# An adaLN + mixture-of-LoRA kernel in Strassen form: a second block on two levels, modulation in place, seeds in PSUM

## The chip, the cores and the metric

One core of one Trainium2 chip. The time is what the device needs for one execution, in microseconds (us); before the change three runs gave a median of 265.66 (265.64 to 265.94). Profiles come from single executions under the hardware profiler. Engines in the profile: PE is TensorE's matmuls, PEld its weight loads, DVE is VectorE, ACT is ScalarE, POOL is GpSimd, SP is SyncE, which here only issues DMAs.

## The reference

All in float32; x is 64 batches of 64 rows of 512.

```python
q_emb = relu(cond_1024 @ W3 + b3)                       # one row of 512 per batch
v = (64 * x + x.sum(axis=1, keepdims=True)) * q_emb[:, None, :]
y = relu(v @ W2 + b2)                                   # first wide product, 512 x 512
base = y @ W_base + b_base                              # second wide product, 512 x 512
shared = (y @ A_s) @ B_s                                # rank 16
gates = softmax(y @ W_router + b_router)                # 6 experts, the best two are kept
routed = sum over experts of w_e * ((y @ A_r[e]) @ B_r[e])
out = x + base + shared + routed
```

## The kernel before

**Blocks.** The 4096 rows are worked in NB = 4 blocks of 16 batches (1024 rows). Features lie on the partitions: a block of x is a tile of 128 partitions x 4 chunks c of features x 2 halves h of the rows x 512 rows. Half 0 has the first 32 rows of each batch, half 1 the others. A block goes through four stages: modulation (x to v), the first wide product (v to y), `ph` (the gate and low-rank products of y, 118 columns), and the second wide product, with the routed part added and the result sent out (`second`).

**Seven products.** Both wide products are Winograd's form of Strassen's scheme: row halves and feature halves make a 2 x 2 of 2 x 2, and seven products of half size take the place of eight. `weight_sums` makes the four sums of weights and `row_sums` the four sums of rows (DVE). `product(ps, i, j, ...)` is product i for output columns j (two j): two matmuls over 512 columns, four records in the trace, 1.72 us. Before the change, block 0 takes half of its rows without sums (`first_mixed`), blocks 1 and 2 take seven products (`first_seven`), and block 3 takes the scheme on two levels (`first_inner`): each of the seven outer products o is again seven inner ones n, 49 matmuls over 256 columns (`q(n, t)`, t counts the outer products in the list `order`). There the common parts of the inner results are carried within PSUM: `seed_y` and `seed_z` copy one bank's half to another with ScalarE, and later matmuls add to it.

**Buffers.** PSUM has eight banks: six for the wide products (`ps_p`), two for `ph` and `pt` (`ps_h`). A bank is asked for with each `ps_p.tile`; one that was used before waits for its last reader. x has three buffers in SBUF and v two; temporaries for results (`temps`: u, u22, u21, u12) have one each.

**Order of the work.** Each engine works its instructions in the order of the program text; there is no scheduler. Modulation of block k+1 runs in the gaps of block k: `prepare(k + 1)` puts its steps in a list `behind`, and `fill(n)` and `share()` in the code of block k take the next steps out. A step is in the main four activations of ScalarE (one per batch) for one chunk, with the next chunk's sums on DVE in front (`sums`: a scaling, a reduction over 1024 elements, a multiplication). `second` takes what is left in nine shares. `prepare_inner` adds the sums that the two-level form needs (inner_t of weights, inner_s of rows).

**Second product.** For each j, product 1 (`x`) is copied to SBUF (L654), added to product 6 (`y`) by DVE (L658), and GpSimd adds x to that three times (L662). `add_r` adds product 7 (`z`). `pt` transposes the weighted low-rank results (`hw`), ScalarE copies them to hwT, and `routed` adds their products to the banks. `finish` (L674) adds bias and remainder and sends 128 x 512 out through SP. The residual x comes from the tile of x, which is why v has its own.

**Loads.** SP issues all loads first, those of x_1 and x_2 at once, and x_3 behind block 0's outputs.

Of the kernel before, what the change touches and what calls it, by code (L numbers as in the profile page):

```python
# [27 lines left out]
NQ = Q // P  # L28
G = E + 1
# [5 lines left out]
def adaln_ffn(ctx: ExitStack, tc: tile.TileContext, xa, x0, x1, head, w3, w2, wb, a, bcat, br, outT):  # L35
# [12 lines left out]
    vpool = ctx.enter_context(tc.tile_pool(name="v", bufs=2))  # L48
    mid = ctx.enter_context(tc.tile_pool(name="mid", bufs=1))
    tmp = ctx.enter_context(tc.tile_pool(name="tmp", bufs=1))  # L50
    tmp1 = ctx.enter_context(tc.tile_pool(name="tmp1", bufs=1))
# [4 lines left out]
    outTv = outT.rearrange("k c h p t -> p c k h t")  # L56
    xs, vs, ss = {}, {}, {}

    def load_x(k):
        xs[k] = xpool.tile([P, NC, 2, TB], F32, tag="x", name=f"x_{k}")  # L60
        for c in range(NC):
            nc.sync.dma_start(xs[k][:, c].rearrange("p h t -> p (h t)"), x1[k - 1, c])
# [4 lines left out]

    def rows(k, f, h):

        return first_rows(f)[:, :, h] if k == 0 else split(xs[k][:, f, h])  # L70

    def split(t, g=2):
        return t.rearrange("p (g n) -> p g n", g=g)
# [50 lines left out]
    load_x(2)  # L124
# [9 lines left out]
    def weight_sums(w, name):  # L134
# [11 lines left out]
        return {1: b11, 2: b21, 3: b22, 4: t[3], 5: t[0], 6: t[1], 7: t[2], "sums": all_t}, steps  # L146

# [25 lines left out]
    def modulate(k):  # L173


        vs[k] = v = vpool.tile([P, NC, 2, TB], F32, tag="v", name=f"v_{k}")
        vsum = small.tile([P, NC, BB], F32, tag="vsum", name=f"vsum_{k}")
        nq = small.tile([P, NC, BB], F32, tag="nq", name=f"nq_{k}")

        def sums(c):  # L180
            xc = xs[k][:, c].rearrange("p h (b n) -> p b h n", n=NH)
            q = q_sb[:, c, ts(k, BB)]
            nc.vector.tensor_scalar(nq[:, c], q, float(N), None, ALU.mult)
            nc.vector.tensor_reduce(vsum[:, c, :], xc, AX.XY, ALU.add)  # L184
            nc.vector.tensor_tensor(vsum[:, c, :], vsum[:, c, :], q, ALU.mult)  # L185

        def batches(c, lo, hi):
            for b in range(lo, hi):
                nc.scalar.activation(  # L189
                    v[:, c, :, ts(b, NH)], xs[k][:, c, :, ts(b, NH)], AF.Identity,  # L190
                    bias=vsum[:, c, b : b + 1], scale=nq[:, c, b : b + 1],
                )

        n = BB // 4
        parts = [(c, lo) for c in range(NC) for lo in range(0, BB, n)]
        steps = [lambda: sums(0)]
        for m, (c, lo) in enumerate(parts):
            if lo == 0 and c + 1 < NC:
                steps.append(lambda c=c, lo=lo: (sums(c + 1), batches(c, lo, lo + n)))
            else:  # L200
                steps.append(lambda c=c, lo=lo: batches(c, lo, lo + n))
        return steps
# [39 lines left out]
    def row_sums(a, name, cols=slice(0, TB)):  # L242

        a11, a12, a21, a22 = a[:, :KH, 0, cols], a[:, KH:, 0, cols], a[:, :KH, 1, cols], a[:, KH:, 1, cols]
        all_s = mid.tile([P, 4, KH, TB], F32, tag=name, name=name)
        s = [all_s[:, i, :, cols] for i in range(4)]
        steps = [
            lambda: nc.vector.tensor_tensor(s[0], a21, a22, ALU.add),
            lambda: nc.vector.tensor_tensor(s[1], s[0], a11, ALU.subtract),
            lambda: nc.vector.tensor_tensor(s[2], a11, a21, ALU.subtract),  # L250
            lambda: nc.vector.tensor_tensor(s[3], a12, s[1], ALU.subtract),
        ]
        return {1: a11, 2: a12, 3: s[3], 4: a22, 5: s[0], 6: s[1], 7: s[2], "sums": all_s}, steps

    def temps(name):
        return {n: tmp.tile([P, KH, TB], F32, tag=n, name=f"{n}_{name}") for n in ("u", "u22", "u21", "u12")}
# [3 lines left out]
    def fill(n):  # L260
        for _ in range(min(n, len(behind))):
            behind.pop(0)()

    def prepare(k):
        behind.extend(modulate(k))
        ss[k], steps = row_sums(vs[k], "s")
        behind.extend(steps)
        if k == NB - 1:
            prepare_inner(k)

    def prepare_inner(k):


        vectors = nc.vector.tensor_tensor
        t_flat = xpool.tile([P, NC, 2, TB], F32, tag="x", name="inner_t").rearrange("p c h t -> p (c h t)")
        at = {i: n for n, i in enumerate((5, 6, 7, 4, 1, 2, 3))}
        inner_t = t_flat[:, : 4 * 7 * P].rearrange("p (n o m) -> p n o m", n=4, o=7)

        def t_of(o, n):
            w, a = t2[o], at[o]  # L280
            b = {1: w[:, 0, :P], 2: w[:, 1, :P], 3: w[:, 1, P:]}
            return b[n] if n in b else inner_t[:, {5: 0, 6: 1, 7: 2, 4: 3}[n], a]

        w_low = w2_sb.rearrange("p (o k) m -> p o k m", k=KH)
        groups = ((slice(0, 4), lambda c, m: t2["sums"][:, :, c, ts(m, P)]),
                  (slice(4, 6), lambda c, m: w_low[:, :, c, ts(m, P)]),
                  (slice(6, 7), lambda c, m: t2[3][:, c, ts(m, P)].unsqueeze(1)))
        t_steps = []
        for o, b in groups:
            t = [inner_t[:, n, o] for n in range(4)]  # L290
            t_steps += [
                lambda t=t, b=b: vectors(t[0], b(0, 1), b(0, 0), ALU.subtract),
                lambda t=t, b=b: vectors(t[1], b(1, 1), t[0], ALU.subtract),
                lambda t=t, b=b: vectors(t[2], b(1, 1), b(0, 1), ALU.subtract),
                lambda t=t, b=b: vectors(t[3], b(1, 0), t[1], ALU.subtract),
            ]
        for n, step in enumerate(t_steps):
            m, other = 2 + n, behind[2 + n]
            behind[m] = lambda step=step, other=other: (other(), step())

        R2 = TB // 2
        s = {}

        def places():
            s["sums"] = vpool.tile([P, NC, 2, TB], F32, tag="v", name="inner_s").rearrange(
                "p c h t -> p (c h t)").rearrange("p (n o t) -> p n o t", n=4, o=4)
            s["first"] = small.tile([P, 4, 1, R2], F32, tag="inner_s1", name="inner_s1")

        def late_places():
            late = mid.tile([P, 4, KH, TB], F32, tag="sy", name="inner_late").rearrange("p n k t -> p (n k t)")  # L310
            s["late"] = late[:, : 8 * R2].rearrange("p (n o t) -> p n o t", n=4, o=2)
            s["e3"] = late[:, 8 * R2 : 12 * R2].rearrange("p (j t) -> p j t", j=KH)

        sources = (("first", lambda c, r: vs[k][:, c, 0, ts(r, R2)].unsqueeze(1)),
                   ("sums", lambda c, r: ss[k]["sums"][:, :, c, ts(r, R2)]),
                   ("late", lambda c, r: vs[k][:, KH + c, :, ts(r, R2)]))
        s_steps = [places]
        for g, a in sources:
            s_steps += [
                lambda g=g, a=a: vectors(s[g][:, 0], a(0, 1), a(1, 1), ALU.add),  # L320
                lambda g=g, a=a: vectors(s[g][:, 1], s[g][:, 0], a(0, 0), ALU.subtract),
                lambda g=g, a=a: vectors(s[g][:, 2], a(0, 0), a(0, 1), ALU.subtract),
                lambda g=g, a=a: vectors(s[g][:, 3], a(1, 0), s[g][:, 1], ALU.subtract),
            ]
        behind.extend(s_steps[:-4])
# [3 lines left out]
        def s_of(o, n):  # L329
# [7 lines left out]
        inner.update(t=t_of, s=s_of, e3=lambda: s["e3"], late=[late_places] + s_steps[-4:])  # L337
# [4 lines left out]
    def first_mixed(y):  # L342
# [3 lines left out]
        vs[0] = v = vpool.tile([P, NC, 2, TB], F32, tag="v", name="v_0")  # L346
# [516 lines left out]
```

## Time and profile before

The profiled execution took 265.05 us: its span from first to last instruction is 263.3, and 1.75 lie around it.

| what | us |
|---|---|
| median of three runs | 265.66 |
| profiled execution / its span | 265.05 / 263.3 |
| TensorE's first `py` matmul starts, last matmul ends | 5.75, 259.3 |
| block 0: `ph` starts, second product starts | 33.4, 40.5 |
| block 1: first product, `ph`, second product start | 72.6, 96.6, 104.2 |
| block 2: the same | 136.0, 160.0, 167.6 |
| block 3: the same | 199.4, 220.4, 227.9 |

How to read it: the page counts each engine's busy time; windows give the same for any stretch, so that a stage of one block can be laid beside that of another. A timeline row gives start, duration, engine, line, operation, output and inputs, count, and in brackets how long the engine had been idle and what it waited for. "The chain of waits" follows the work that ended last back from its end. Some durations worth knowing here:

| row | what | mean ns |
|---|---|---|
| L189 ACT | one batch's modulation, 128x64 | 429 (16 in a row: 5.41 us) |
| L184 DVE | row reduction, 128x1024 | 1212 |
| L662 POOL | add of x, 128x512 | 1356 |
| L674 DVE | bias, PSUM and remainder, 128x512 | 748 |
| L654 ACT | copy out of PSUM, 128x512 | 581 |
| L486, L489 ACT | seed copy within PSUM, 128x256 | 357, 363 |
| x loads, SP | 512 KB | 7.1 us to landing |
| outputs, SP | 256 KB | 2.0 us to landing |

### The profile page before, as it was taken

What the parts mean: (1) busy time and instruction counts of PE and PEld (TensorE: products, weight loads), DVE (VectorE), ACT (ScalarE), POOL (GpSimd) and SP (SyncE); (2) the same over time, 40 slices, a digit from 0 to 9 for tenths busy, and PEclk for the clock granted to TensorE, in tenths of its full rate; (3) what the DMA queues carried; (4) which work ended last, traced back from release to release, by engine and by line L of the source; (5) the groups of instructions that cost most, each with busy time, mean ns of one, the idle gap of its engine ahead of it and who ended that gap; (6) DMA issues with size and microseconds to landing.
All of it is one profiled execution on the core that took longest, in us unless ns stands there. A gap on an engine that the chain in (4) does not pass through costs nothing.

```text
span 263.3 us, 2789 instructions
## 1 busy us (share of the span) xinstructions
PE 257.9 (98%) x920; PEld 148.8 (57%) x920; DVE 168.4 (64%) x296; ACT 119.2 (45%) x318; POOL 43.8 (17%) x45
## 2 busy tenths in 40 slices
PE   7999999999999999999999999999999999999995
PEld 3756895454444458444444447744446889845542
DVE  2896889636755448714667776876989566872422
ACT  2499389594018992245003998246004328101000
POOL 1000000570000000435000000055600070045300
PEclk9999999999999999999999999999999999999999
DMA  6999300004362000002220000000332000000323
GB/s 200 364 346 410 123 0 0 0 2 159 115 249 113 0 2 0 1 0 88 111 105 18 0 0 0 2 0 0 113 128 80 1 4 0 0 4 0 120 90 109
DMA packets 10303, 20.13 MB, mean 76 GB/s; under 512 B 1216, under 2 KB 3008, under 8 KB 10288
## 3 DMA queue, kind: packets, MB, share of 16 engines
q1 hardware_dynamic: 10000, 19.82, 20.7%
q8 instruction: 7, 0.11, 0.2%
q10 hardware_dynamic: 288, 0.13, 0.2%
q14 instruction: 8, 0.07, 0.1%
HBM read 11.56 MB, written 8.39 MB: 76 GB/s over the span
## 4 chain that ended last, share of the span: by engine, by line
PE 91%; ACT 5%; DMA 2%; DVE 1%; SPq 0%; issue 0%; DVEq 0%
PE oz L150 11%; PE ox L150 10%; PE ph L801 10%; PE ow L150 9%; PE py L354 5%; PE yw L150 5%; PE yz L150 5%; PE oy L150 5%; PE ia L480 5%; PE ow L668 5%; PE yx L150 4%; PE ib L480 4%; PE yy L150 3%; ACT v L189 3%; PE ox L668 3%; PE oz L668 3%
## 5 line engine op out<-in xcount | busy, mean ns | idle before, releaser
L189 ACT ACTIVATE v<-x,vsum,nq 128x64 f32<-128x64 f32 x192 | 66.3, 429 | 6.7 <-DVE vsum L185 6.7
L662 POOL TENSOR_TENSOR u_o<-u_o,x 128x512 f32<-128x512 f32 x24 | 31.9, 1356 | 178.3 <-DVE u_o L658 178.3
L801 PEld LDWEIGHTS ph<-a_sb,y 128*128 128x128 f32 x256 | 29.5, 192 | 1.8 <-issue 1.0
L801 PE MATMUL ph<-a_sb,y 128*128 128x118 f32 x256 | 29.9, 276 | 0.3 <-ACT y L340 0.3
L150 PE MATMUL ox<-y,wb_sb 128*128 128x512 f32 x64 | 29.5, 593 | 0.0
L340 ACT ACTIVATE y<-u,head_sb 128x512 f32<-128x512 f32 (+1 forms) x26 | 15.9, 633 | 8.8 <-DVE u L412 3.6
L150 PEld LDWEIGHTS ox<-y,wb_sb 128*128 128x128 f32 x64 | 11.8, 190 | 12.9 <-issue 12.9
L674 DVE SCALAR_TENSOR_TENSOR u_o<-ow,head_sb,u_o 128x512 f32<-128x512 f32 x14 | 10.5, 748 | 8.5 <-PE ow L668 8.2
L658 DVE TENSOR_TENSOR u_o<-oy,op 128x512 f32<-128x512 f32 x8 | 5.5, 688 | 15.5 <-PE oy L150 15.5
L354 PE MATMUL py<-v,w_sb 128*128 128x512 f32 (+1 forms) x40 | 14.4, 510 | 0.9 <-DMA w_sb<-in_w_dram 0.9
L150 PE MATMUL oz<-y,tb 128*128 128x512 f32 x32 | 15.1, 595 | 0.0
L150 PE MATMUL yx<-v,w_sb 128*128 128x512 f32 x32 | 15.0, 592 | 0.0
L150 PE MATMUL oz<-sy,tb 128*128 128x512 f32 x32 | 15.0, 592 | 0.0
L150 PE MATMUL oy<-sy,tb 128*128 128x512 f32 x32 | 15.0, 592 | 0.0
L437 ACT COPY p<-yx 128x512 f32<-128x512 f32 x4 | 2.3, 576 | 27.7 <-PE yx L150 27.7
L184 DVE TENSOR_REDUCE vsum<-x 128x16 f32<-128x1024 f32 x12 | 14.5, 1212 | 0.0
L654 ACT COPY op<-ox 128x512 f32<-128x512 f32 x8 | 4.7, 581 | 19.1 <-PE ox L150 19.1
L150 PE MATMUL ow<-sy,tb 128*128 128x512 f32 x28 | 13.2, 593 | 0.0
L150 PE MATMUL ow<-sy,wb_sb 128*128 128x512 f32 x28 | 13.2, 592 | 0.0
L674 DVE SCALAR_TENSOR_TENSOR x<-ox,head_sb,x 128x512 f32<-128x512 f32 x8 | 6.0, 749 | 10.6 <-PE ox L668 10.6
L486 ACT COPY ib<-ia 128x256 f32<-128x256 f32 x7 | 2.5, 357 | 21.2 <-PE ia L480 21.2
L237 ACT ACTIVATE v<-x,vsum,nq 128x64 f32<-128x64 f32 x32 | 10.9, 427 | 1.7 <-DVE vsum L235 1.7
(170 smaller groups left out, 413.3 us busy)
## 6 DMA issues: line engine op xcount, KB each, us to landing
x<-in_x_dram SPq DMA_DIRECT2D x12, 512.0 KB, 7.1
out_dram<-u_o SPq DMA_DIRECT2D x22, 256.0 KB, 2.0
out_dram<-x SPq DMA_DIRECT2D x8, 256.0 KB, 2.1
x<-in_x_dram SPq DMA_DIRECT2D x7, 256.0 KB, 6.0
w_sb<-in_w_dram SPq DMA_DIRECT2D x4, 256.0 KB, 5.7
wb_sb<-in_wb_dram SPq DMA_DIRECT2D x4, 256.0 KB, 5.0
w_sb<-in_w_dram SPq DMA_DIRECT2D x1, 384.0 KB, 4.3
out_dram<-u_o SPq DMA_DIRECT2D x2, 192.0 KB, 1.9
```

What stands on the lines that cost most here:

```text
L150: nc.tensor.matmul(ps, w[i][:, c, ts(j, P)], s[i][:, c, :], start=start and c == 0, stop=c == KH - 1, skip_group_check=True,)
L184: nc.vector.tensor_reduce(vsum[:, c, :], xc, AX.XY, ALU.add)
L189: nc.scalar.activation(v[:, c, :, ts(b, NH)], xs[k][:, c, :, ts(b, NH)], AF.Identity, bias=vsum[:, c, b : b + 1], scale=nq[:, c, b : b + 1],)
L237: nc.scalar.activation(v[:, c, :, ts(b, NH)], batches_of(c, b, b + 1)[:, :, 0], AF.Identity, bias=vsum[:, c, b : b + 1], scale=nq[:, c, b ...
L340: nc.scalar.activation(y[:, f, h, cols], src, AF.Relu, bias=b2_sb[:, f : f + 1])
L354: nc.tensor.matmul(p[:, :, lo * NH : hi * NH], w2_sb[:, c, ts(f, P)], v[:, c, :, lo * NH : hi * NH], start=(c == 0 and lo == 0), stop=(c = ...
L480: nc.tensor.matmul(bank[b, t][:, cols], inner["t"](o, n), inner["s"](o, n), start=n == 1, stop=True, skip_group_check=True,)
L658: nc.vector.tensor_tensor(us[j], ps["y", j], p1s[j], ALU.add)
L662: nc.gpsimd.tensor_tensor(split(t[j], x.shape[1]), split(us[j], x.shape[1]), x, ALU.add)
L668: nc.tensor.matmul(ps[name, j], bcat_sb[:, ts(f, P)], hw, start=False, stop=True, skip_group_check=True)
L674: nc.vector.scalar_tensor_tensor(add, split(p, g), bb_sb[:, f : f + 1], add, ALU.add, ALU.add)
L801: nc.tensor.matmul(ph[:, h * NS + s, :HC], y[:, c, h, ts(s, P)], a_sb[:, c, :], start=(c == 0), stop=(c == NC - 1),)
```

## The change

- **First product of block 2** is `first_inner` too, with its own row sums; the weight sums inner_t are constants and are made during block 1. `first_inner` itself now has fills (two units ahead of step t = 2, two in each step), since block 3 is prepared behind it. The four sums of the group `late` are GpSimd's and come first.
- **Modulation in place**: v is the tile of x. A unit is two activations instead of four; chunks go in the order 0, 2, 1, 3, and the row sums are made in halves.
- **The residual** is loaded a second time: `load_rows(k)`, behind the first product, into the four temporaries (512 KB each). `with_x` adds bank and bias to it.
- **Seeds**: in `first_seven` and `second` ScalarE copies a bank into a fresh bank and the next product adds to it, in place of a copy to SBUF and adds on DVE and GpSimd. Relus read PSUM where they can. The order of products in `second` is new.
- **Block 0**: the accumulators of j = 0 and j = 1 share a bank (`px`, and `y`, `w`, `z` of the seven products).
- x_2 is loaded behind block 0's modulation, x_3 behind `load_rows(0)`.

```diff
     def load_x(k):
         xs[k] = xpool.tile([P, NC, 2, TB], F32, tag="x", name=f"x_{k}")
-        for c in range(NC):
-            nc.sync.dma_start(xs[k][:, c].rearrange("p h t -> p (h t)"), x1[k - 1, c])
+        for c in CHUNKS:
+            nc.sync.dma_start(xs[k][:, c].rearrange("p h t -> p (h t)"), x1[k, c])
...
-        vs[k] = v = vpool.tile([P, NC, 2, TB], F32, tag="v", name=f"v_{k}")
+        vs[k] = v = xs[k]
...
+        def batch(c, b):
+            x = v[:, c, :, ts(b, NH)]
+            nc.scalar.activation(x, x, AF.Identity, bias=vsum[:, c, b : b + 1], scale=nq[:, c, b : b + 1])
...
     def fill(n):
         for _ in range(min(n, len(behind))):
-            behind.pop(0)()
+            for step in behind.pop(0):
+                step()
-    def prepare(k):
+    def prepare(k, also=()):
...
+        early, late = row_steps(slice(0, 1)), row_steps(slice(1, 2))
+        units = [[sums[CHUNKS[0]]]]
+        for i, c in enumerate(CHUNKS):
+            for b in range(0, BB, 2):
+                unit = batches[c][b : b + 2]
+                if b == 0 and i + 1 < NC:
+                    unit.insert(0, sums[CHUNKS[i + 1]])
+                if i == KH and b % 4 == 2:
+                    unit.append(early[b // 4])
+                units.append(unit)
+        for n, step in enumerate(also):
+            units[2 + n].append(step)
+        behind.extend(units + [[step] for step in late])
+        if k > 1:
+            behind.extend([step] for step in prepare_inner(k))
...
+        late = [late_places] + steps("late", lambda c, r: vs[k][:, KH + c, :, ts(r, R2)], nc.gpsimd)
...
     def first_mixed(y):
...
-                    px[j], w2_sb[:, c, ts(j, P)], v[:, c, 0, other], start=(c == 0), stop=(c % KH == KH - 1),
+                    px[:, j], w2_sb[:, c, ts(j, P)], v[:, c, 0, other],
+                    start=(c == 0 and j == 0), stop=(c % KH == KH - 1),
...
-                    nc.scalar.copy(p1[j], px[j])
+                    nc.scalar.copy(p1[j], px[:, j])
...
+        load_x(2)
...
+        banks = [ps_p.tile([P, KH, cols], F32, tag="pp", name=f"y{n}_0") for n in "ywz"]
...
     def first_seven(k, y):
         s = ss[k]
-        prepare(k + 1)
+        prepare(k + 1, inner_steps)
...
             product(px, 1, j, t2, s)
-            nc.scalar.copy(p1, px)
-            product(py, 6, j, t2, s)
-            nc.vector.tensor_tensor(u, py, p1, ALU.add)
-            fill(1)
+            nc.scalar.copy(py, px)
             product(pw, 5, j, t2, s)
-            nc.vector.tensor_tensor(r, pw, u, ALU.add)
-            fill(1)
-            product(pz, 7, j, t2, s)
+            nc.scalar.copy(r, pw)
+            product(py, 6, j, t2, s, start=False)
+            nc.scalar.copy(pz, py)
+            product(px, 2, j, t2, s, start=False)
+            nc.scalar.copy(u, py)
+            fill(2)
+            relu(y, f1, 0, px)
+            product(pz, 7, j, t2, s, start=False)
             nc.vector.tensor_tensor(r, pz, r, ALU.add)
+            fill(2)
             relu(y, f2, 1, r)
-            fill(2)
-            product(px, 2, j, t2, s, start=False)
-            relu(y, f1, 0, px)
             product(pw, 3, j, t2, s, start=False)
             nc.vector.tensor_tensor(r2, pw, u, ALU.add)
+            fill(2)
             relu(y, f2, 0, r2)
-            fill(1)
             product(pz, 4, j, t2, s, start=False)
-            nc.vector.tensor_tensor(r1, pz, u, ALU.add)
-            relu(y, f1, 1, r1)
-            fill(1)
+            relu(y, f1, 1, pz)
+            fill(2)
...
     def first_inner(k, y):
-        late = inner["late"]
-        late.pop(0)()
+        for step in inner[k]["late"]:
+            step()
+        prepare(k + 1)
...
-        for step in late:
-            step()
         q(2, 0)
...
         q(2, 1)
+        fill(2)
         for t in range(2, 7):
...
             take_w5(t)
+            fill(1)
             q(3, t - 1)
...
                 relus(p1, 0, 0)
+            fill(1)
...
+    def load_rows(k):
+        res = {}
+        for n, (f, h) in zip(pair_tags[2:3] + pair_tags[:2] + pair_tags[3:], ((1, 0), (1, 1), (0, 0), (0, 1))):
+            res[f, h] = tmp.tile([P, KH, TB], F32, tag=n, name=f"x{n}_{k}")
+            nc.sync.dma_start(
+                res[f, h], x1[k, f * KH : (f + 1) * KH, :, ts(h, TB)].rearrange("c p t -> p c t")
+            )
+        return res
...
+        def seed(name, source, j):
+            nc.scalar.copy(bank(name, j), ps[source, j])
...
+        def with_x(name, j, f, h):
+            t = row(f, h)
+            nc.vector.scalar_tensor_tensor(t, ps[name, j], bb_sb[:, f : f + 1], t, ALU.add, ALU.add)
+            return t
...
+        def leave(p, f, h, add, cols=slice(0, TB), queue=nc.sync):
+            nc.vector.tensor_tensor(add[:, cols], p[:, cols], add[:, cols], ALU.add)
+            queue.dma_start(outT[k, f, h, :, cols], add[:, cols])
...
         prod(1, 0, "x")
-        copy_p1(0)
-        prod(6, 0, "y")
-        add_u(0)
+        seed("y", "x", 0)
+        prod(1, 1, "x")
+        seed("y", "x", 1)
+        prod(6, 0, "y", start=False)
+        seed("z", "y", 0)
+        prod(2, 0, "x", start=False)
...
+        u12[0] = with_x("y", 0, KH, 0)
         share()
-        prod(7, 0, "z")
-        prod(2, 0, "x", start=False)
-        add_r(0)
-        prod(1, 1, "x")
-        copy_p1(1)
+        prod(7, 0, "z", start=False)
+        u22[0] = with_x("z", 0, KH, 1)
+        prod(6, 1, "y", start=False)
+        seed("z", "y", 1)
+        u12[1] = with_x("y", 1, KH + 1, 0)
         share()
-        prod(4, 0, "z", start=False)
-        prod(6, 1, "y")
-        add_u(1)
-        share()
-        prod(7, 1, "z")
+        prod(2, 1, "x", start=False)
+        prod(7, 1, "z", start=False)
+        u22[1] = with_x("z", 1, KH + 1, 1)
...
+        share()
+        prod(4, 0, "z", start=False)
         prod(5, 0, "w")
-        add_r(1)
...
-        elif k < NB - 1:
+        elif k == 1:
             first_seven(k, y)
         else:
             rest = first_inner(k, y)
+        res = load_rows(k)
+        if k == 0:
+            load_x(3)
...
         if k == 0:
-            fill(4)
-        second(k, y, ph)
-        if k + 3 < NB:
-            load_x(k + 3)
+            fill(8)
+        second(k, y, ph, res)
```

## The prediction

> **What bounds the kernel now.** I read part 1 of the page first, then the same stages of different blocks side by side in windows, then the timelines around every place where TensorE idles.
>
> ```profile
> PE 257.9 (98%) x920; PEld 148.8 (57%) x920; DVE 168.4 (64%) x296; ACT 119.2 (45%) x318; POOL 43.8 (17%) x45
> ```
>
> TensorE is busy for 257.9 of 263.3 us, and 3.9 of the rest lie behind its last matmul. No other engine is near a bound as a sum, so the change can gain in two ways only, by fewer matmul columns or by the few waits of TensorE, and it loses by each new wait of TensorE. Columns of the windows below: stretch, its length, busy time (instructions) of PE, PEld, DVE, ACT, POOL, granted clock, DMA share, GB/s.
>
> ```profile
> 33.40:40.55 7.15, 7.15 (x66) 7.15 (x65) 6.47 (x11) 6.56 (x20) 0.00 (x0) 1.00 0.00 0
> 40.55:72.60 32.05, 32.05 (x83) 14.43 (x82) 20.61 (x35) 17.97 (x53) 8.67 (x7) 1.00 0.17 58
> 96.60:104.20 7.60, 7.43 (x66) 7.25 (x65) 5.42 (x5) 3.59 (x10) 0.00 (x0) 1.00 0.01 2
> 104.20:136.00 31.80, 31.80 (x82) 14.49 (x82) 17.00 (x28) 9.12 (x25) 8.67 (x7) 1.00 0.16 58
> 136.00:160.00 24.00, 24.00 (x58) 10.60 (x57) 16.26 (x31) 17.21 (x45) 0.00 (x0) 1.00 0.03 11
> 160.00:167.60 7.60, 7.43 (x66) 7.25 (x65) 5.61 (x6) 3.60 (x10) 0.00 (x0) 1.00 0.01 2
> 199.40:228.00 28.60, 28.60 (x164) 25.62 (x163) 20.45 (x41) 13.16 (x34) 5.00 (x4) 1.00 0.05 16
> ```
>
> The rows are: block 0's gate matmuls (`ph`), its second product; block 1's `ph`, its second product; block 2's first product with seven products, its `ph`; block 3's first product on two levels together with its `ph`. The reader sees three differences between equal work. Block 2 takes 24.00 + 7.60 = 31.60 where block 3 takes 28.60. `ph` takes 7.60 in blocks 1 and 2 but 7.15 in block 0. Block 0's second product takes 32.05, block 1's 31.80.
>
> **What goes, by those rows.** Block 2 takes the form of block 3: 31.60 - 28.60 = **3.00** (about 2.55 from 24.5 instead of 28 matmuls of 512 columns, 0.45 from the wait in `ph`). Block 1 keeps seven products; its 0.45 in `ph` is this wait (shown for block 2):
>
> ```profile
> 160.24 1.43 ACT L189 ACTIVATE v<-x,vsum,nq 128x64 f32<-128x64 f32 x4
> 161.56 0.71 ACT L340 ACTIVATE y<-u,head_sb 128x512 f32<-128x512 f32 x1
> 162.32 5.39 PE L801 MATMUL ph<-a_sb,y 128*128 128x118 f32 x46 [0.17 <-ACT y L340]
> ```
>
> The last relu stands on ScalarE behind four modulation activations and, before them, behind DVE's add. In the new order that relu reads PSUM directly and stands ahead of the last fill, and the one before it is behind four activations that fit between: with the third product from the end done 3.43 before the end T, DVE's add ends at T-2.7, relu to T-2.05, four activations (0.334 from start to start, 16 in 5.41) to T-0.7, relu to T. The first `ph` group needs it 0.65 later. So **0.45** goes, and row sums and gate follow with room. Block 0's 0.25 is product 4 of j=0, which waited for DVE's add behind GpSimd's L662; it now comes two products later, and L662 is gone: **0.25**. Sum of gains 3.70.
>
> **What is added, one by one.** Seeds in the second product: a 128x512 ScalarE copy out of PSUM took 581 ns (L654; 256 wide, to PSUM 357, to SBUF 378, so 0.55 to 0.6). Each seed has a product of 1.72 between its source and its user. Gate's exponential stands ahead of the first seed; it ended 1.0 behind `ph` in blocks 1 and 2, and 2.65 in block 0: there copy to 3.25, and TensorE asks at 3.44. Cost 0, but the cover in block 0 is 0.2; a later gate is paid one to one. The seed of z for j=1 is queued behind the first share's eight activations (2.76): from 5.8 to 8.6 behind `ph`, and its source ends at 10.3. Cover 1.7, cost 0. hwT's copies are behind the second share, which ends at 13.7, and `pt` at 14.6: 0. ScalarE's four copies and four relus per half of block 1 (about 4.4) plus 14 to 16 activations (5) fit in 12.0 of matmuls: 0.
>
> The reload of x: four 512 KB loads per block on SP, each behind the release of a temporary; the nearest row, 512 KB loads of x, landed in 7.1. The first piece is asked for about 12 us behind the start of `ph`, its buffer is free at or before that start, and no output is queued behind a load that waits long. 8 MB more at a mean of 76 GB/s: 0 (bounds 0 and 1). The moved loads of x for blocks 2 and 3 go out behind x_0's last reader (22.4) and behind block 0's first product (about 36), at least 35 us before block 2 and 3 read them. Modulation in place is the same instruction, `leave` as a plain add is no dearer than L674's 749 ns: 0. The twelve weight sums move into block 1 (0.28 to 0.69 each, 6 in all) and the row sums are cut in halves (8 x 0.69 for 4 x 1.22): DVE is busy 12 of 24 there, 0.
>
> Block 0's **shared banks** are the first place where rule and row part. `px` for j=0 and j=1 now lie in one PSUM bank.
>
> ```profile
> 22.41 0.81 ACT L367 COPY p<-yx 128x256 f32<-128x256 f32 x2
> 22.84 1.59 PEld L361 LDWEIGHTS yx<-v,w_sb 128*128 128x128 f32 x8 [0.43 <-ACT p L367]
> ```
>
> With a bank each, the first copy ran beside j=1's matmuls and TensorE went on after it, at 22.84. By this row the cost is 0. The Trainium skill (PSUM — Partial Sum Buffer, section on bank collisions) says that two engines must be kept apart on a whole bank, whatever columns they touch, so both copies come after both matmuls (22.81) and the next matmul after both copies: 22.85 + 0.37 + 0.37 = 23.57 instead of 22.84, **0.7**. Here the rule speaks against the change, and block 3 agrees with it: its seed copy of the low half of a bank starts at 205.03, behind the matmul into the other half (from 204.40), not behind its own. I take 0.7.
>
> **Fills in block 2's two-level product.** Write S for its start (199.53 in block 3, in the chain of waits). The ninth matmul ends at S+4.2, DVE's take of it at S+4.6. Behind it DVE now has two chunk sums (0.17 + 1.21 + 0.17, about 1.45 each), and ScalarE's first two activations need the first: S+6.05. Then two activations (0.67), a copy (0.27), the seed (0.36): S+7.4. TensorE wants that seed at S+6.75 (206.29 in block 3). Cost **0.66**. Later steps fit: per step ScalarE has two seeds and four activations, about 1.9, in 3.0 of matmuls. At the end two activations (0.67) stand ahead of the relus of e3, which had 0.3 to spare: **0.3**.
>
> **`late` moves to GpSimd**, the second such place. Four 128x512 adds (nearest L575: 1.27 each) start there when `sy` is free, at S-0.86; DVE then still has two 1024-wide sums and the last `leave` (0.75): the product before the last ends at S-2.6, its `leave` at S-1.85, and the ninth share puts three sums of 1.22 (L321 to L323) behind it. Whose bank matters: the third step opens the fifth and sixth bank at S+4.6, one of which that `leave` must have freed.
>
> ```profile
> 180.62 5.69 POOL L662 TENSOR_TENSOR u_o<-u_o,x 128x512 f32<-128x512 f32 x3 [4.22 <-DVE u_o L658]
> 180.95 2.02 DVE L248 TENSOR_TENSOR s<-v 128x1024 f32<-128x1024 f32 x1 [0.41 <-ACT v L189]
> 189.29 1.21 DVE L251 TENSOR_TENSOR s<-v,s 128x1024 f32<-128x1024 f32 x1
> ```
>
> Beside GpSimd the wide add took 2.02 instead of 1.21 (L249 and L250: 1.69, 2.28; mean +0.8). By this row the two sums run from S-0.65 to S+3.4, `leave` to S+4.15: free in time, cost 0. The skill (SBUF — State Buffer, Who interferes with whom) calls it an exclusive lock: an add with two SBUF inputs waits for a whole GpSimd add. Taking turns, `leave` ends at S+4.85, and blocks 2 and 3 wait 0.25 each. I take the row; the rule's 0.5 stays in the range.
>
> **Sum.** 3.70 - 0.70 - 0.66 - 0.30 = 2.04. The profiled execution took 265.05 (span 263.3 and 1.75 around it), so 263.0. The median of the runs shown is 265.66, 0.61 above the profiled one; against it I forecast **263.6**.
>
> **Rivals.**
> - *The costs don't come* (the banks are kept apart by columns only, DVE gets to its sums early): 265.66 - 3.70 = 262.0. Against it: the 205.03 row. Chance 0.12.
> - *ScalarE sets the pace of block 2's first product.* An activation alone lasts 429 ns, not 334. From one seed to the next stand 0.36 + 2 x 0.43 = 1.22, against 1.29 of matmuls (three of 0.43), so any further 0.1 to 0.3 per handover is TensorE's wait. Over five steps 1.7 at most: 265.3, no change. For it, thin cover; against it, 16 activations in 5.41. Chance 0.13.
> - *Slower: GpSimd holds DVE in both two-level blocks.* GpSimd starts first, and if three of its adds go ahead of DVE's two sums, these begin at S+2.95, end at S+5.4, `leave` at S+6.1. The third step then waits 1.5 in block 2 and in block 3, and block 2's sums come 0.4 later still: 3.4 more, 267.0. It eats the whole gain once `leave` ends at about S+5.5. For it: POOL was 1.5 times slower in that stretch too, so both wait; against it: DVE never waited for more than one add there. I put other waits on seeds (block 0's 0.2 of cover) here as well. Chance 0.25.
> - The forecast itself, with its own range 262.5 to 264.9 by the bounds above: 0.50.
>
> A measurement of this kernel can tell about 0.2%, 0.53 us, from no change. Faster by more: the forecast and the first rival, less the edge, 0.60. Within: 0.13. Slower: 0.27. The range 261.7 to 266.7 takes in all but the upper part of the slower case.
>
> **What would show it.** Right: block 2's first product with `ph` at 29.5 to 30 in the windows, `ph` of block 1 at 7.15, about 0.7 of TensorE idle at 22.8 to 23.6 ended by ACT L367's copy, one wait of some 0.7 for the seed in block 2's third step, seconds at 31.8. Wrong: TensorE waits for ScalarE copies inside the second products, for a bank at S+4.6 behind DVE's last `leave`, or for a residual load.

## The result, and the profile after

The changed kernel takes **267.03 us** (median of four runs, 266.89 to 267.27) where the kernel before took 265.65 beside it: ratio 1.0053, 95% interval 1.0036 to 1.0070. The forecast was 263.6; the change is slower by 1.4. (In the later rounds the kernel before took 267.3 to 267.7 in 16 of 89 executions, for a reason that no trace here shows; its medians stay at 265.63 to 265.66, and the table of stages below accounts for the 1.4.) The profiled execution took 267.05 (span 265.0). Part 1 of its page:

```profile
PE 256.7 (97%) x962; PEld 157.2 (59%) x962; DVE 177.8 (67%) x327; ACT 133.7 (50%) x356; POOL 31.3 (12%) x33
```

TensorE has less to do than before (256.7 against 257.9), yet the span grew by 1.7: the gain in matmuls was given back as waits. The windows tell in which stages (columns as before: stretch, length, busy time of PE, PEld, DVE, ACT, POOL, clock, DMA share, GB/s):

```profile
41.64:73.45 31.81, 31.81 (x83) 14.43 (x82) 21.87 (x39) 19.83 (x57) 1.27 (x1) 1.00 0.43 161
97.48:104.61 7.13, 7.13 (x65) 7.13 (x64) 4.72 (x4) 2.21 (x6) 0.00 (x0) 1.00 0.67 220
136.42:167.57 31.15, 29.11 (x164) 25.46 (x162) 25.67 (x47) 20.28 (x56) 11.44 (x8) 1.00 0.23 78
199.37:229.77 30.40, 28.84 (x163) 25.54 (x162) 22.81 (x38) 13.16 (x34) 12.25 (x8) 1.00 0.25 84
```

The rows are block 0's second product, block 1's `ph`, and the first product with `ph` of blocks 2 and 3. The first two are full and as short as forecast. The last two do the same matmuls as block 3 did before in 28.57, and TensorE stands still in both. By the starts of TensorE's stages, in us (block 0's first product counted from its first `yx` matmul to `ph`):

| stage | before | after | difference |
|---|---|---|---|
| block 0, `yx` to `ph` | 15.89 | 16.59 | +0.70 |
| block 0, second product | 32.05 | 31.81 | -0.24 |
| block 1, `ph` | 7.56 | 7.13 | -0.43 |
| block 2, first product and `ph` | 31.60 | 31.15 | -0.45 |
| block 3, first product and `ph` | 28.57 | 30.40 | +1.83 |
| other second products (three) | 95.66 | 95.65 | 0 |

The sum is +1.41, the difference of the medians 1.38. (The time up to the first `yx` differs by 0.42 more, but that part, in which the first loads land, ranged from 17.67 to 18.62 among the profiled executions below whatever the edit, and is left out. The last second product is counted to the end of the last matmul, 259.98 before and 261.80 after; the 259.3 given for before in the table further up is 0.7 too early.)

**Block 0.** The shared bank costs what was forecast. From the timeline (start, duration, engine, line, operation, in brackets the idle time before and what ended it):

```profile
23.27 0.65 ACT L365 COPY p<-yx 128x256 f32<-128x256 f32 x2 [0.49 <-PE yx L358]
...
23.97 2.00 PE L358 MATMUL yx<-v,w_sb 128*128 128x256 f32 x8 [0.74 <-ACT p L365]
```

Both copies now come after all four matmuls into the bank, and the next matmul after both copies.

**Block 3.** DVE and GpSimd from the end of block 2, in the timeline:

```profile
198.81 1.27 POOL L313 TENSOR_TENSOR inner_late<-x 128x512 f32<-128x512 f32 x1 [13.62 <-PE ow L170]
199.16 2.00 DVE L314 TENSOR_TENSOR inner_s<-inner_s,s 128x1024 f32<-128x1024 f32 x1
200.16 2.13 POOL L314 TENSOR_TENSOR inner_late<-inner_late,x 128x512 f32<-128x512 f32 x1
201.08 2.28 DVE L315 TENSOR_TENSOR inner_s<-s 128x1024 f32<-128x1024 f32 x1
202.25 2.25 POOL L315 TENSOR_TENSOR inner_late<-x 128x512 f32<-128x512 f32 x1
...
205.50 0.68 DVE L694 TENSOR_TENSOR xu<-ow,xu 128x512 f32<-128x512 f32 x1
206.10 0.41 DVE L471 TENSOR_TENSOR u<-ib,u 128x256 f32<-128x256 f32 x1
...
206.56 0.70 PE L480 MATMUL ib<-x,inner_t 128*128 128x256 f32 x2 [1.56 <-DVE u L471]
```

The reader is to see a zip: each DVE add ends about 1.1 after the GpSimd add before it, and each GpSimd add about 1.1 after the DVE add before it, though nothing in the data ties them. An add that takes 1.22 alone lasts 2.28 here. The last `leave` of block 2 (205.50, the add with which a result leaves its bank for the output) is queued behind three such adds, take_22(0) (206.10, the add with which DVE takes a result of the first outer product out of its bank) behind `leave`, and TensorE's q(4, 0) waits for that: wanted at 204.84, it starts at 206.56. (Counted from S, the start of the block's first matmul in the timeline, wanted at S+5.47; the S of the prediction, from the chain of waits, is 0.16 later, and its times are quoted below with 0.16 added.) The wait is 1.72, and the pair of matmuls behind a stall takes 0.53 to the next instead of 0.43.

**Block 2, third step:**

```profile
141.11 0.41 DVE L471 TENSOR_TENSOR u<-ib,u 128x256 f32<-128x256 f32 x1
...
141.66 1.21 DVE L204 TENSOR_REDUCE vsum<-x 128x16 f32<-128x1024 f32 x1
...
143.00 0.17 DVE L203 TENSOR_SCALAR nq<-q_sb 128x16 f32<-128x16 f32 x1
...
143.12 0.77 ACT L209 ACTIVATE x<-x,vsum,nq 128x64 f32<-128x64 f32 x2 [2.25 <-DVE vsum L205]
...
144.05 0.37 ACT L486 COPY ib<-ia 128x256 f32<-128x256 f32 x1
...
144.47 0.70 PE L480 MATMUL ib<-inner_s,inner_t 128*128 128x256 f32 x2 [1.12 <-ACT ib L486]
```

Take, chunk sum, two activations, a copy, the seed, and then the matmul that adds to it: the chain that was forecast, with 1.29 of wait where 0.66 was.

**Block 2, near the end**, a place the prediction does not have:

```profile
153.90 1.27 POOL L578 TENSOR_TENSOR u<-u,u 128x512 f32<-128x512 f32 x1
153.98 1.21 DVE L203 TENSOR_SCALAR nq<-q_sb 128x16 f32<-128x16 f32 x1
...
155.11 1.21 DVE L204 TENSOR_REDUCE vsum<-x 128x16 f32<-128x1024 f32 x1
...
158.17 0.70 PE L480 MATMUL ib<-s,inner_t 128*128 128x256 f32 x2 [0.92 <-DVE inner_late L471]
```

The last chunk sum of block 3's modulation stands in front of DVE's takes. Its 16-element scaling, 0.17 at 143.00, lasted 1.21 here: it ended together with the GpSimd add beside it, at 155.2. TensorE's matmul, wanted at 157.09, came 1.08 late. By these rows, as an estimate, 1.04 of the 1.08 is the scaling's wait for GpSimd; this add (L578) is not one of the `late` ones and is in the kernel before too. No run tests the scaling by itself.

### The profile page after: what moved, and what is told of

Its sections match the earlier page's. It is cut to its first block, busy times and chain, and to the rows that moved or that the text cites. A ratio compares the mean times of both kernels' runs of the same rounds, so it can differ in the third digit from the quotient of the medians.

```text
span 265.0 us, 2971 instructions
## 1 busy us (share of the span) xinstructions
PE 256.7 (97%) x962; PEld 157.2 (59%) x962; DVE 177.8 (67%) x327; ACT 133.7 (50%) x356; POOL 31.3 (12%) x33
## 4 chain that ended last, share of the span: by engine, by line
PE 82%; DVE 10%; ACT 4%; issue 2%
PE ph L810 11%; PE ox L170 10%; PE oz L170 8%; PE ia L480 6%; PE ib L480 6%; PE py L351 5%; PE ow L170 5%; PE oy L170 5%; PE yw L170 4%; PE yz L170 4%; ACT x L209 4%; PE ow L673 3%; PE yx L170 3%; PE yy L170 2%; PE idle L181 2%
## 5 line engine op out<-in xcount | busy, mean ns | idle before, releaser
L209 ACT ACTIVATE x<-x,vsum,nq 128x64 f32<-128x64 f32 x192 | 66.8, 432 | 2.3 <-DVE vsum L205 2.3
L737 POOL TENSOR_TENSOR hwd<-hwT 112x512 f32<-112x512 f32 x4 | 5.5, 1363 | 173.3 <-ACT hwT L735 144.9
L669 DVE SCALAR_TENSOR_TENSOR xu<-oz,head_sb,xu 128x512 f32<-128x512 f32 x16 | 12.0, 750 | 13.7 <-PE oz L170 9.5
L337 ACT ACTIVATE y<-u,head_sb 128x256 f32<-128x256 f32 (+1 forms) x26 | 14.4, 600 | 7.4 <-DVE u L412 4.0
L471 DVE TENSOR_TENSOR u<-ib,u 128x256 f32<-128x256 f32 x28 | 11.1, 419 | 7.3 <-PE ib L480 7.3
L694 DVE TENSOR_TENSOR xu<-ow,xu 128x512 f32<-128x512 f32 x14 | 9.6, 689 | 7.4 <-PE ow L673 7.0
L669 DVE SCALAR_TENSOR_TENSOR xu<-ox,head_sb,xu 128x512 f32<-128x512 f32 x8 | 6.0, 749 | 11.6 <-PE ox L673 11.6
L480 PE MATMUL ib<-inner_s,inner_t 128*128 128x256 f32 x40 | 12.0, 387 | 1.1 <-ACT ib L486 1.1
L471 DVE TENSOR_TENSOR u<-ia,u 128x256 f32<-128x256 f32 (+1 forms) x24 | 10.8, 463 | 3.1 <-ACT u L518 1.7
L661 ACT COPY oz<-oy 128x512 f32<-128x512 f32 x8 | 4.6, 570 | 15.6 <-PE oy L170 15.6
```

What stands on the lines that cost most here:

```text
L209: nc.scalar.activation(x, x, AF.Identity, bias=vsum[:, c, b : b + 1], scale=nq[:, c, b : b + 1])
L337: nc.scalar.activation(y[:, f, h, cols], src, AF.Relu, bias=b2_sb[:, f : f + 1])
L471: add = lambda o, a, b: nc.vector.tensor_tensor(o, a, b, ALU.add)
L480: nc.tensor.matmul(bank[b, t][:, cols], t_side(o, n), s_side(o, n), start=n == 1, stop=True, skip_group_check=True,)
L669: nc.vector.scalar_tensor_tensor(t, ps[name, j], bb_sb[:, f : f + 1], t, ALU.add, ALU.add)
L694: nc.vector.tensor_tensor(add[:, cols], p[:, cols], add[:, cols], ALU.add)
```

## The experiments

All are edits of the changed kernel; ratios are to the kernel before, timed beside them, and savings are against the changed kernel's 267.03. The theory after the two traces: (A) GpSimd's late adds and DVE's adds exclude each other, which makes block 3's wait; (C) the chunk sums in block 2's two-level product make both waits there. The rival to both is that DVE and ScalarE are simply too full in these stages.

**e1: the late adds behind the first take.** GpSimd reads one column that take_22(0) writes, so that its four adds follow it.

```diff
     def first_inner(k, y):
-        for step in inner[k]["late"]:
-            step()
+        inner[k]["late"][0]()
         prepare(k + 1)
...
         take_22(0)
+        hold = small.tile([P, 1], F32, tag="hold", name=f"hold_{k}")
+        nc.gpsimd.tensor_tensor(hold, p1[:, 1, TB - 1 :], p1[:, 1, TB - 1 :], ALU.add)
+        for step in inner[k]["late"][1:]:
+            step()
         q(2, 1)
```

> GpSimd's four adds of the group late start only behind DVE's take_22(0), held by a one-column add that reads its result; same adds, same engine. Theory A (GpSimd's adds and DVE's 1024-wide adds take turns, so DVE's last leave and take_22(0) come late in both two-level blocks): the wait of 1.7 us in block 3 goes, and about 0.4 of the 1.3 us wait in block 2's third step; median 264.8 to 265.2. Rival B (DVE is late in block 3 because ScalarE's activations end late, at 192.1, and its row sums behind them): the wait in block 3 keeps 1.0 us or more, median 266.2 or above.

Measured: **264.79**, ratio to before 0.9955 (0.9939 to 0.9971), 2.24 less than the changed kernel. Block 3 takes 28.57 again; block 2's third step waits 0.97 instead of 1.29. The same DVE adds in this kernel's timeline:

```profile
200.07 1.22 DVE L315 TENSOR_TENSOR inner_s<-s 128x1024 f32<-128x1024 f32 x1
201.20 1.22 DVE L316 TENSOR_TENSOR inner_s<-s,inner_s 128x1024 f32<-128x1024 f32 x1
202.34 0.68 DVE L697 TENSOR_TENSOR xu<-ow,xu 128x512 f32<-128x512 f32 x1
```

No DVE work was taken away, only its company: the durations fall from 2.28 to 1.22, and `leave` starts at S+3.20 instead of S+6.13. A is shown, and rival B falls; that the turns alone are not enough for block 3's wait is the matter of e6 and e7.

**e2: block 3's chunk sums moved** into block 1's second product, with a second buffer for `vsum` and `nq`.

```diff
...
-        sums, batches = modulate(k)
+        sums, batches = early_sums.pop(k) if k in early_sums else modulate(k)
...
         left = [9]
+        ahead, batches = modulate(NB - 1) if k == 1 else ({}, None)
+        ahead = list(ahead.values())
+        if k == 1:
+            early_sums[NB - 1] = ({c: lambda: None for c in CHUNKS}, batches)
 
         def share():
+            if ahead and left[0] < 9:
+                ahead.pop(0)()
```

> The four chunk sums (DVE) for block 3 are taken out of the fills of block 2's two-level product and done in block 1's second product, one in each of the shares 2 to 5; vsum and nq get a second buffer. Theory C (both waits of block 2, 1.3 us in the third step and 1.1 us near the end, come from these chunk sums ahead of DVE's takes and of ScalarE's activations): both go, median 264.6 to 265.0, block 3 keeps its 1.7. Rival D (the activations themselves hold up the seed): only the 1.1 goes, the third step still waits 0.6 or more, median about 265.9.

Measured: **264.88**, ratio 0.9972 (0.9961 to 0.9983), 2.15 less. Both waits inside block 2's first product are gone (21.00 up to `ph`, where 23.58 were); block 3 keeps its 1.83. The two matmuls that had waited, in this kernel's timeline, now follow the one before without idle time:

```profile
143.35 0.59 PE L481 MATMUL ib<-inner_s,inner_t 128*128 128x256 f32 x2
...
155.87 0.59 PE L481 MATMUL ib<-s,inner_t 128*128 128x256 f32 x2
```

C is shown, and rival D falls. Block 2 with `ph` takes 29.16, not 28.57: a remainder of 0.59 at `ph`, which the wait near the end had hidden.

**e3: `px` in two banks**, as before the change.

```diff
-                    px[:, j], w2_sb[:, c, ts(j, P)], v[:, c, 0, other],
-                    start=(c == 0 and j == 0), stop=(c % KH == KH - 1),
+                    px[j], w2_sb[:, c, ts(j, P)], v[:, c, 0, other],
+                    start=(c == 0), stop=(c % KH == KH - 1),
...
-        px = ps_p.tile([P, KH, cols], F32, tag="pp", name="yx_0")
+        px = [ps_p.tile([P, cols], F32, tag="pp", name=f"yx_0_{j}") for j in range(KH)]
...
```

> Only px of block 0 gets two banks again, one for each j. If the shared bank costs what the trace shows at 23.3 to 24.0, TensorE waits 0.7 us less there and the median is 266.3; if something else is late there next, 266.9 to 267.1.

Measured: **266.49**, ratio 1.0020 (1.0004 to 1.0036), 0.54 less; TensorE runs all twelve `yx` records in a row and block 0 takes 15.90. The kernel leaves out a part of the computation. Its engines do the same work (962 matmuls, 327 instructions of DVE, 356 of ScalarE, as in the changed kernel), so its time can be compared. What is left out is presumably this: where such a half-filled bank is used again later, the half of ScalarE's seed that its tile did not cover is not added. The Trainium skill (PSUM — Partial Sum Buffer, The four PSUM rules) gives a reason: a group's first matmul marks the whole bank as unwritten, only matmuls mark columns as written, and a later matmul overwrites unmarked columns whatever ScalarE put there. That fits, and would be why the change shares banks in block 0, but no run here tests it. The profiled execution, the slowest of eight (267.36), lost 0.43 in block 2, which the edit does not touch; the last section comes back to it.

**e4: e1, e2 and e3 together** (with e3's omission).

> The three edits together. If they are separate waits of one bound engine they add up, less some 0.4 us that the first two share: 267.0 - 2.1 - 2.3 - 0.7 + 0.4 = about 262.3, 3.3 below the kernel before. If a wait takes the place of those removed (the bank of the last leave, the relus at the end), 263 to 264.5.

Measured: **262.48**, ratio 0.9880 (0.9867 to 0.9892). The three parts save 4.93 by themselves and 4.55 together: they are separate causes but for about 0.4, and 0.32 of that is the part of block 2's third step that e1 and e2 both remove.

**e9: the same three mends with the whole computation.** `px` stays in one bank; its second pair of matmuls is issued ahead of the last chunk's eight `py` records, so that the copies lie beside those. (The edits of e1 and e2, which are in it too, are not shown again.)

```diff
-            if c == KH - 1:
-                for j in range(KH):
-                    nc.scalar.copy(p1[j], px[:, j])
...
                 modulate_group(v, vsum, c, lo, hi)
+                if c == NC - 1:
+                    without_sums(1)
                 for f in range(NC):
...
             if c == NC - 1:
+                for j in range(KH):
+                    nc.scalar.copy(p1[j], px[:, j])
                 modulate_scalar(v, vsum, nq, c, half, BB)
-            if c > 1:
-                without_sums(c - 2)
+            if c == 2:
+                without_sums(0)
```

> The changed kernel with three mends that keep the whole computation: GpSimd's late adds behind the first take (as in e1), block 3's chunk sums in block 1's second product (as in e2), and in block 0 the shared px bank kept, but its second pair of matmuls issued ahead of the eight py records of the last chunk, so that ScalarE's two copies run beside those. Theory (the three waits are independent, and the bank wait is only a matter of what lies behind it): 262.2 to 262.8, no TensorE wait at the px bank. Rival (a bank shared costs wherever it is put: the copies, ahead of the last chunk's eight activations now, push block 0's row sums and its first product with sums by 0.65): 262.9 to 263.3, with a TensorE wait for DVE's sums at about 25.

Measured: **262.60**, ratio 0.9876 (0.9844 to 0.9907). The bank wait is gone. The rival holds in part: the two copies stand ahead of eight activations, the row sums come later, and TensorE waits 0.32 for them at 25.13 (0.16 in e11, not at all in e10, the same code here; what makes the difference stays open).

**e6: block 2 back to seven products**, the rest as changed (two lines not shown see to it that the sums of the two-level form are made for block 3 alone).

```diff
...
-        elif k == 1:
+        elif k < NB - 1:
             first_seven(k, y)
```

> The changed kernel with block 2's first product by seven products again, nothing else. Theory (block 2's waits of 1.29 and 1.08 eat all of the 2.5 of the matmuls against seven products in the new order, which take 31.16 with the gate products in block 1; block 3's 1.7 stays, since it is made in block 3): 266.8 to 267.2, the same as the changed kernel. Rival (the two-level form in block 2 also makes block 3's wait, by leaving more preparation over for block 2's second product): 265.2 to 266.0, with block 3's first wait below 0.5.

Measured: **265.01**, ratio 0.9968 (0.9952 to 0.9984). My theory falls, its rival holds. Block 2 takes 31.17, the same as the 31.15 on two levels with its waits; but block 3's 1.83 is gone, though GpSimd's adds are where they were. The modulation's activations (windows limited to that line, so that the columns are stretch, length, ScalarE's busy time and count, clock, DMA share, GB/s; the first row is the changed kernel, the second e6, each for the later part of block 2's second product):

```profile
178.50:199.37 20.87, 11.48 (x34) 1.00 0.20 75
```

```profile
179.20:200.10 20.90, 8.83 (x26) 1.00 0.23 85
```

`first_inner` takes out twelve of block 3's steps, `first_seven` sixteen. On two levels block 2 leaves eight more activations to its second product. Counted from S of block 3 they end at S-7.30 where they ended at S-9.90 in e6, 2.6 later; DVE's row and inner sums follow later, and three wide adds instead of two meet GpSimd. In e6 `leave` starts at S+4.09, in the changed kernel at S+6.13.

**e7: at least six units in the second product's first two shares.**

```diff
-            fill(-(-len(behind) // left[0]))
+            fill(max(-(-len(behind) // left[0]), 6 if left[0] > 7 else 0))
```

> The changed kernel with at least six units in each of the second product's first two shares, so that modulation ends earlier and DVE's row sums and inner sums of block 3 start earlier; GpSimd's late adds stay where they are. Theory (block 3's wait comes from two things together, the late start of DVE's sums at S-0.4 and the turns with GpSimd): sums start 2 us earlier, the wait of 1.7 falls below 0.5, 265.3 to 265.9. Rival 1 (the turns alone decide): 266.8 to 267.1. Rival 2 (twelve activations ahead of the seed of z for j=1 use up its cover of 1.7): new TensorE waits of 0.5 or more for ScalarE in the second products, three of them, 267.5 or more.

Measured: **265.52**, ratio 0.9987 (0.9972 to 1.0002), 1.5 less than the changed kernel. Block 3 is at 28.58 with two of its adds still at 2.28, and its `leave` starts at S+4.09:

```profile
201.42 2.28 DVE L316 TENSOR_TENSOR inner_s<-s,inner_s 128x1024 f32<-128x1024 f32 x1
...
203.63 0.68 DVE L694 TENSOR_TENSOR xu<-ow,xu 128x512 f32<-128x512 f32 x1
```

Rivals 1 and 2 fall; the second products take 31.80 to 31.81 (the last 32.03), as in the changed kernel. Block 3's wait needs both the turns and the late start; either removed alone removes it. But the edit reaches block 2 as well, and there the profiled execution loses 0.40 (31.55 for 31.15). DVE is done with its wide adds earlier, GpSimd's last add falls beside the scaling of the chunk sum instead, and the third step waits 1.69 instead of 1.29:

```profile
140.90 1.03 DVE L203 TENSOR_SCALAR nq<-q_sb 128x16 f32<-128x16 f32 x1
...
144.63 0.70 PE L480 MATMUL ib<-inner_s,inner_t 128*128 128x256 f32 x2 [1.53 <-ACT ib L486]
```

1.83 less 0.40 is 1.43, near the 1.5 by which the median fell.

**e5: the late adds on DVE**, at the same place.

```diff
-        late = [late_places] + steps("late", lambda c, r: vs[k][:, KH + c, :, ts(r, R2)], nc.gpsimd)
+        late = [late_places] + steps("late", lambda c, r: vs[k][:, KH + c, :, ts(r, R2)])
```

> The changed kernel with the four late adds on DVE instead of GpSimd, at the same place of the program; nothing else. Theory (an add on GpSimd takes its whole length away from DVE's two-input adds, so the four adds gave DVE no relief): DVE's adds go back to 1.2 each, its last leave in block 3 ends at about S+3.8 instead of S+6.1, and the first take 0.5 earlier than in the changed kernel although DVE does four adds of 0.6 more: block 3 gains 0.5, block 2 loses 0.3 (take at S+5.0), 266.5 to 267.1. Rival (GpSimd did relieve DVE, by the part that overlaps): DVE has 2.4 more to do in both blocks ahead of the first take, 268.5 to 271.

Measured: **266.57**, ratio 1.0042 (1.0028 to 1.0056), 0.46 less than the changed kernel, with intervals that overlap. DVE has four adds more to do (0.61 from start to start). It reaches take_22(0) of block 3 at S+6.31 instead of S+6.73, and that of block 2 at S+5.06 instead of S+4.69. So GpSimd relieved DVE by 0.37 in block 2 and held it up by 0.42 in block 3: the stages change by +0.23 and -0.40, and the rest of the 0.46 is not in these two. Over both blocks, sending these adds to GpSimd at that place gave DVE no relief. The theory holds, its rival falls.

**e10: block 2 on seven products, with e1 and e9's block 0.**

> Block 2's first product by seven products again (block 3 alone on two levels), with GpSimd's late adds behind the first take and the px copies hidden. It has no block 2 waits of the two-level form to lose. Theory (the two-level form is worth the 2.55 of its matmuls, and the changed kernel lost that to the waits around it): about 2.5 over e9, 264.7 to 265.2. Rival (the form is worth little even without waits, since its edges cost as much): within 1.0 of e9, 262.5 to 263.5.

Measured: **264.37**, ratio 0.9943 (0.9923 to 0.9963): 1.77 over e9, between theory and rival, since e9 still lost 0.59 at `ph` and 0.32 at `yy`. Neither block 2 nor block 3 waits in e10.

**e11: e9 without the last fill of the two-level product**, its unit going to the second product.

```diff
                 relus(p1, 0, 0)
-            fill(1)
+            if t < 6:
+                fill(1)
```

> e9 with one thing more: the last unit of modulation in the two-level product (two activations, with or without a sum, ahead of the relus of e3) goes to the second product's shares instead. In e9 block 2's gate products take 8.16 up to the second product, block 3's, without fills, 7.57; the two activations stand ahead of the relus that the first gate products need. Theory (these activations are the 0.59): 262.0, block 2's ph part 1.78 like block 3's. Rival (the relus are late for DVE's adds before them, not for the activations): 262.6, no change.

Measured: **261.74**, ratio 0.9862 (0.9847 to 0.9877), 3.9 below the kernel before. `ph` of block 2 takes 7.57 again where it took 8.16: the two activations were the 0.59, as the theory has it. (The median fell by 0.86 from e9's; 0.16 more is the shorter wait at `yy`, and the rest is not traced.) In its windows blocks 2 and 3 are now alike, without a wait:

```profile
136.33:164.90 28.57, 28.57 (x163) 25.59 (x162) 18.71 (x37) 19.73 (x54) 10.17 (x9) 1.00 0.24 84
196.71:225.28 28.57, 28.57 (x163) 25.59 (x162) 20.44 (x39) 13.16 (x34) 10.15 (x9) 1.00 0.26 90
```

Against e10 that is 2.63 in the medians, and 31.17 - 28.57 = 2.60 in the windows: this is what the two-level form is worth in block 2 once its surroundings let it.

## Why the prediction was wrong

By its own steps, measured beside forecast (minus is a gain):

| step | forecast | measured |
|---|---|---|
| block 2 on two levels, before costs | -3.00 | -3.03 where nothing waits (e11: 31.60 to 28.57) |
| block 1's `ph`; block 0's second product | -0.45; -0.25 | -0.43; -0.24 |
| seeds, reload, moved loads, modulation in place | 0 | 0 (second products 31.80 to 31.81, but the last) |
| `px` in a shared bank | +0.70 | +0.70 |
| chunk sums before the seed, block 2's third step | +0.66 | +1.39 (1.29, and 0.10 for the restart) |
| relus of the tile `e3` behind the last fill | +0.30 | hidden behind the next row; 0.59 where that is gone (runs e2, e9) |
| "Later steps fit" | 0 | +1.18 near block 2's end |
| GpSimd's `late`, block 2 / block 3 | 0 / 0 | 0 at its own place, but 0.32 of the third step's 1.29 (e1) / +1.83 |

The gains and the rule on the shared bank held to 0.03. Two steps failed, and a third was mis-sized.

*"I take the row."* The row and the rule of the Trainium skill (SBUF — State Buffer, Who interferes with whom: an exclusive lock) stood side by side, and I took the mean of three add lengths (+0.8) from a stretch where GpSimd had three adds of its own. The rule of turns is what both blocks show: forecast by it, `leave` ends at S+5.01, measured S+4.77 in block 2. But the rule alone would have given 0.25 for each block. What made 1.83 is the second half of the same step, *"DVE then still has two 1024-wide sums"*: that was read off the kernel before, whose block 2 took seven products and drained more of the modulation behind them. On two levels block 2 drains twelve steps instead of the sixteen of seven products in the new order (e6), so in block 3 a third wide add met GpSimd, and `leave` came 2.04 later than in block 2. The step that I costed by a row of before was moved by another part of the change.

*"Later steps fit."* I counted ScalarE's time per step and left out that the units carry chunk sums for DVE; the one that falls near the end stands ahead of a take that TensorE is about to need. As estimated above from the rows, nearly all of its cost is GpSimd's hold on that sum's scaling.

*The third step,* forecast at 0.66, has the right chain, chunk sums included, and a wrong size: 1.29. GpSimd is one reason. It held up `leave` and with it DVE's take, which began at S+4.69 (S+4.37 in e1; forecast to be done by S+4.76), and the first scaling lasted 0.31 beside its add, so that the first activation came at S+6.70 instead of S+6.21. The other is in the working: S and the time at which TensorE wants the seed (206.29) were taken from the chain of waits, the take from the timeline, where TensorE asks at 206.13. With one origin for both the step would have come to about 0.8. With the adds out of the way (e1) the wait is 0.97.

Of the rivals, the one with GpSimd holding DVE named the mechanism and, at 267.0, the time. The agreement of the time is partly luck: it has 1.5 in each block, where block 3 had 1.83 and block 2's larger loss came from the chunk sums; and it has three GpSimd adds going ahead of DVE's two sums, where the two engines took turns and DVE had three sums to do. Its place was not quite right either: `leave` decides less by the bank that it frees (the seed that needs it, at 206.27, came in time after it) than by standing ahead of take_22(0) in DVE's queue. By the rows of block 3, TensorE waits once `leave` starts after S+4.4 (it wants q(4, 0) at S+5.47 and starts it 1.06 after `leave`). The rival of ScalarE setting the pace did not show: with the sums moved (e2) no wait is left between the steps.

## What to carry to other kernels

When one part of a change alters how much background work a stage drains, every arrival time behind it has to be worked out again, and the rows of the kernel before no longer hold for it; the wait may turn up a block later. DVE's adds with two SBUF inputs and GpSimd's adds ran one at a time here: moving such work from DVE to GpSimd pays only where DVE is doing something else, so place it by DVE's schedule and not by when its inputs are ready. In a queue with tight handovers, look at what each filler puts on every engine, not on the one that is counted.

## What the hardware showed that was not expected

- **Which of DVE's operations wait for GpSimd** is sharply divided. Beside GpSimd's 128x512 adds (1.27 alone): the add with two SBUF inputs 2.28 instead of 1.22, the scaling of 16 elements 1.21 instead of 0.17; the reduction over 1024 stayed at 1.21, adds with one PSUM input at 0.41 and 0.68. The Trainium skill (SBUF — State Buffer, Who interferes with whom) divides them in this way, and this case agrees with all four.
- **The turns are not fixed.** In e3's profiled execution GpSimd's first late add of block 2 waited through three DVE adds, 3.71 in all, and DVE's next two adds kept their 1.22, where the changed kernel, with the same start relative to S, alternated from the first. GpSimd then ran later, the scaling at the third step lasted 1.04 instead of 0.31, and the step's wait was 1.71 instead of 1.29. What decides the turn stays open.
- **A stall costs a little more than its length**: behind each of the three, the first pair of 128x256 matmuls took 0.53 to the next pair instead of 0.43. It is not the length of the stall: the pair at 201.14 of the changed kernel's trace, which started 0.04 late behind a copy of ScalarE, took 0.53 as well. In both the profile shows the weight load waiting with the matmul (at 206.56 the two start together) instead of running ahead of it.
